# Group normalisation and a quantised 3x3 convolution: low parts by row pairs, and three steps on another engine

## The chip, the cores and the metric

The kernel runs on one core of one Trainium2 chip. The metric is the device time of one execution in microseconds (us). The engines are named as in the profile: PE (matmuls, with PEld for its weight loads), DVE (vector), ACT (scalar), POOL (GpSimd) and SP (which issues DMAs).

## What is computed

The input x has 160 images of 128 channels and 32x32 pixels; the weights U come in five sets (N = 5). Images go round the sets: image b*5 + n belongs to set n.

```python
beta, alpha = jnp.max(U), jnp.min(U)
s1 = (beta - alpha) / 3.0
v1 = s1 * floor(U / s1)
s2 = s1 / 5.0
v2 = s2 * floor((U - v1) / s2)
w = (v1 + v2).reshape(OUT_CH * N, IN_CH, 3, 3)
xb = _gn(x).reshape(B // N, N * C, H, W)      # 32 groups of 4 channels, each image for itself
act = conv(xb, w, stride 1, padding 1, feature_group_count=N)
out = x + act.reshape(x.shape)
```

## The kernel before, in words

Channels lie on the 128 partitions; an image is 1024 fp32 elements on each. The kernel goes through the images set by set, 32 images each. Four images make a chunk, loaded by one DMA of 2 MB from SP's queue (`load`, L304), 16 images ahead, and stored from ACT's queue after its fourth image (`residual`, L439).

The weights become small whole numbers m = 5*k1 + k2 in fp16, exact, with their scale kept for the end. `make_row` (L350) makes three of the nine taps of a set: 17 DVE operations on 384 elements (`quantise`, L93, and `floor_div`, L79; each yields after every operation, so that they can be dealt out), three transposes on PE (L364) and a copy by ACT (L366). Three such pieces make a set. For the first set they stand in the start; for each later one, from the 13th image of the set before on, four steps follow each image (`later`, L555 to L558), which takes 13 images.

An image passes through these steps:

- `measure` (L370): DVE's two `bn_stats` and one `bn_aggr` (L149, L150), 12 images ahead. Groups of 2, 2, 4, 4, 4 and then 8 images share what follows: `means` (L152, a matmul that averages the four channels of a group), `deviations` (L160, four small DVE operations), `variances` (L170, a matmul) and `scales` (L173: `ve` on DVE, a power and a product on POOL). Means and deviations fall to one image's turn, variances and scales to the next one's.
- `normalise` (L379): DVE makes z in fp32 (L384), ACT rounds it to fp16 (`hi`, L392).
- `remainder` (L395): DVE takes `lo` = z - `hi`, also fp16 (L398). `hi` + `lo` keep nearly all of z.
- `conv` (L400): for each tap, part (`hi`, `lo`) and half image (16 rows) one matmul of up to 512 columns, so 9 x 2 x 2 = 36, each with its own weight load, all into one pair of PSUM banks (`pc`, three pairs).
- `residual` (L424): DVE adds the scaled `pc` to x in place (L431).

The order of each engine's work is the order of the program text (`manual_schedule`). The loop of `run` (L519) puts for image i: means and variances, `normalise(i + 2)`, the 36 matmuls, `residual(i - 1)`, `remainder(i + 2)`, scales, deviations, one `measure`, four weight steps, a load. The start (L464 to L516) mixes the first set's weights with images 0 to 3 by hand; the first three images get their taps piece by piece as the weights come.

A general version for other weight ranges (`general_path`, L183) stands behind a test and doesn't run with these inputs.

## Time and profile before

| | |
|---|---|
| median of 3 runs | 1296.75 us (1295.84 to 1297.18) |
| profiled execution | 1296.91 us, span 1295.2 us |
| granted PE clock | 0.992 of full speed |
| busy: PE, DVE, ACT, POOL | 1238.0, 883.0, 174.6, 43.4 us |
| matmuls of the convolution (L416) | 5760 |
| DMA | 171.69 MB, mean 133 GB/s |

The span is the part of the time that the trace covers. A row of a group has the line, engine, operation, output and inputs, their shapes, the count, then busy us and mean ns of one, then the idle us just before them and who ended it. A matmul's duration covers its way through the array, in which the next one has begun; how fast they follow each other is read from their starts. In the timeline a row is a start, a length and what ran, like operations merged (x2); in the chain of waits a row is a stretch without a break.

### The profile page before, as it was taken

How to read it: one execution, taken by the hardware profiler on the slowest of the kernel's cores; microseconds unless marked ns; L12 is line 12 of the kernel's file. 1: busy time of each engine (PE TensorE's matmuls, PEld its weight loads, DVE VectorE, ACT ScalarE, POOL GpSimd, SP SyncE). 2: the span in 40 equal slices, each digit the busy share in tenths (PEclk: the TensorE clock that was granted, in tenths of full speed). 3: DMA queues.
4: the chain of work that ended last, by engine and by line, in shares of the span. 5: the costliest groups of instructions: out<-in, count | busy, mean ns of one | idle time of the engine just before them, and what ended most of it. 6: DMA issues, size and time to landing. Idle time of an engine off the chain costs nothing.

```text
span 1295.2 us, 13840 instructions
## 1 busy us (share of the span) xinstructions
PE 1238.0 (96%) x5901; PEld 580.1 (45%) x5901; DVE 883.0 (68%) x1367; ACT 174.6 (13%) x177; POOL 43.4 (3%) x57
## 2 busy tenths in 40 slices
PE   0589999999999999999999999999999999999997
PEld 0234444444444444444444444444444444444443
DVE  7886788855667887656688866657887566555441
ACT  0111111111111111111111111111111111111110
POOL 1000000000000000000000000000000000000000
PEclk9889999999999999999999999999999999999999
DMA  9403333333333333333333333433333333111122
GB/s 379 166 34 151 142 133 150 150 150 130 134 130 131 130 130 130 130 131 130 138 150 152 144 133 142 156 151 133 130 130 130 131 130 130 65 65 66 73 89 102
DMA packets 43270, 171.69 MB, mean 133 GB/s; under 512 B 1472, under 2 KB 1472, under 8 KB 43200
## 3 DMA queue, kind: packets, MB, share of 16 engines
q1 hardware_dynamic: 21600, 85.66, 17.8%
q10 hardware_dynamic: 21600, 85.07, 16.5%
q8 instruction: 48, 0.79, 0.2%
q14 instruction: 22, 0.18, 0.0%
HBM read 86.84 MB, written 83.89 MB: 132 GB/s over the span
## 4 chain that ended last, share of the span: by engine, by line
PE 94%; DVE 5%; DMA 0%; issue 0%; ACT 0%; DVEq 0%
PE pc L416 94%; DVE st L149 1%; DVE ext L323 0%; DVE ext L324 0%; DMA u<-in_L_conv_U_dram 0%; DVE tt L88 0%; DVE tt L89 0%; DVE tt L87 0%; DVE tt L90 0%; DVE k L91 0%; PE pg L156 0%; DVE z L384 0%; PE pg L171 0%; PE pt L364 0%; DVE lo L398 0%; DVE nn L85 0%
## 5 line engine op out<-in xcount | busy, mean ns | idle before, releaser
L416 PEld LDWEIGHTS <-wt 128*128 128x128 f16 x5760 | 565.4, 99 | 648.9 <-issue 7.5
L416 PE MATMUL pc<-hi,wt 128*128 128x496 f16 (+3 forms) x2880 | 850.3, 377 | 0.6 <-ACT wt L366 0.6
L416 PE MATMUL pc<-lo,wt 128*128 128x496 f16 (+3 forms) x2880 | 849.4, 376 | 0.0
L431 DVE SCALAR_TENSOR_TENSOR xt<-pc,s2z,xt 128x1024 f32<-128x1024 f32 (+1 forms) x161 | 205.5, 1277 | 370.4 <-PE pc L416 370.4
L392 ACT CAST hi<-z 128x1024 f16<-128x1024 f32 x160 | 167.2, 1045 | 984.0 <-DVE z L384 948.2
L149 DVE BATCH_NORM_STATS2 st<-xt 128x6 f32<-128x512 f32 x320 | 204.2, 680 | 0.0
L398 DVE TENSOR_TENSOR lo<-z,hi 128x1024 f16<-128x1024 f32 x160 | 194.5, 1216 | 4.0 <-ACT hi L392 4.0
L384 DVE TENSOR_SCALAR z<-xt,gm,rstd 128x1024 f32<-128x1024 f32 x160 | 125.2, 783 | 8.3 <-POOL rstd L180 8.2
L178 POOL TENSOR_TENSOR rstd<-ve,mhalf 128x8 f32<-128x8 f32 (+2 forms) x23 | 35.1, 1527 | 1163.0 <-DVE ve L176 1163.0
L150 DVE BATCH_NORM_AGGREGATE mv<-st 128x2 f32<-128x12 f32 x160 | 33.4, 209 | 5.5
L364 PE MATMUL pt<-ident,m 128*128 128x128 f16 x45 | 5.3, 231 | 19.2 <-DVE m L358 19.2
L366 ACT COPY wt<-pt 128x384 f16<-128x384 f16 x15 | 7.2, 478 | 102.1 <-DMA out_dram<-xt 59.4
L337 PE MATMUL rows<-ident,ext 128*1 128x128 f32 x2 | 0.6, 394 | 19.1 <-DVE ext L328 19.1
L90 DVE TENSOR_TENSOR tt<-tt,nn 128x384 f32<-128x384 f32 x30 | 16.5, 551 | 0.9
L91 DVE TENSOR_TENSOR k<-nn,tt 128x384 f32<-128x384 f32 x30 | 16.3, 544 | 0.7
L364 PEld LDWEIGHTS <-m 128*128 128x128 f16 x45 | 3.9, 106 | 22.2 <-DVE m L358 19.3
L156 PEld LDWEIGHTS pg<-mv,gavg 128*128 128x128 f32 x46 | 9.0, 202 | 8.6 <-DVE mv L150 5.0
L156 PE MATMUL pg<-mv,gavg 128*128 128x8 f32 (+2 forms) x46 | 7.1, 226 | 5.6 <-DVE mv L150 4.8
L171 PEld LDWEIGHTS pg<-dv,gavg 128*128 128x128 f32 x46 | 8.8, 202 | 7.6 <-DVE dv L168 5.2
L171 PE MATMUL pg<-dv,gavg 128*128 128x8 f32 (+2 forms) x46 | 7.3, 231 | 5.0 <-DVE dv L168 5.0
L86 DVE TENSOR_SCALAR nn<-nn 128x384 f32<-128x384 f32 x30 | 10.6, 352 | 0.8
L323 DVE TENSOR_REDUCE ext<-u 128x1 f32<-128x1152 f32 x5 | 6.7, 1344 | 5.1 <-DMA u<-in_L_conv_U_dram 5.1
(60 smaller groups left out, 130.1 us busy)
## 6 DMA issues: line engine op xcount, KB each, us to landing
xt<-in_x_dram SPq DMA_DIRECT2D x39, 2048.0 KB, 7.7
out_dram<-xt ACTq DMA_DIRECT2D x39, 2048.0 KB, 6.6
xt<-in_x_dram SPq DMA_DIRECT2D x4, 512.0 KB, 9.9
u<-in_L_conv_U_dram SPq DMA_DIRECT2D x3, 576.0 KB, 7.7
out_dram<-xt ACTq DMA_DIRECT2D x3, 512.0 KB, 2.6
u<-in_L_conv_U_dram ACTq DMA_DIRECT2D x2, 576.0 KB, 6.8
out_dram<-xt ACTq DMA_DIRECT2D x2, 256.0 KB, 2.9
```

The lines of the kernel that those rows point to most:

```text
L90: yield nc.vector.tensor_tensor(t, t, n, ALU.is_lt)
L91: yield nc.vector.tensor_sub(k, n, t)
L149: self.nc.vector.bn_stats(st[:, h, :], image[:, h * half : (h + 1) * half])
L150: self.nc.vector.bn_aggr(self.mv[:, j, :], st)
L156: self.nc.tensor.matmul(self.pg[:, 0, :], self.gavg, self.mv[:, :, 0], start=True, stop=True)
L171: self.nc.tensor.matmul(self.pg[:, 1, :], self.gavg, self.dv, start=True, stop=True)
L178: nc.gpsimd.tensor_tensor(self.rstd, ve, self.mhalf[:, : self.nb], ALU.pow)
L384: nc.vector.tensor_scalar(z, self.image(i), st.gm[:, j : j + 1], st.rstd[:, j : j + 1], ALU.subtract, ALU.mult,)
L392: nc.scalar.copy(hi.rearrange("p h w -> p (h w)"), z)
L398: self.nc.vector.tensor_sub(lo_flat, z, hi_flat)
L416: nc.tensor.matmul(pc[:, h, r0 - top : r1 - top, c0:c1], self.wts[n, tap // ROW][:, tap % ROW, :], self.pairs[i][part][:, r0 + dh : r1 + d ...
L431: self.nc.vector.scalar_tensor_tensor(xj[:, h], pc[:, h], self.steps.s2z, xj[:, h], ALU.mult, ALU.add)
```

## The change

From image 3 on, the low part is convolved two output rows at a time. With g0, g1, g2 the three taps of a column and x the low rows, the rows 2i and 2i+1 together need g0 on (x[2i-1] - x[2i+1]), -g2 on (x[2i] - x[2i+2]), and half the sum and half the difference of (g0+g1+g2) on (x[2i] + x[2i+1]) and (g0-g1+g2) on (x[2i+1] - x[2i]): four products for two rows, where the taps taken one by one need six. So DVE makes the row differences `d` and the sums and differences `st` (`combinations`), POOL the two weight combinations, ACT the negated g2. PE runs for an image six full-size matmuls on `st` into a bank pair `m` of its own, the 18 direct ones of the high part and twelve half-size ones on `d` (8 rows of 32) into `eo`. ACT brings `m` out as fp16 (`leave`), DVE makes its sum and difference by rows (`pq`, in `add_pairs`), and two matmuls with the scaled identity `up` add them to `eo`. Images 0 to 2 keep the direct form (`conv_direct`), image 2 in the bank pair `m`.

z is made on ACT from POOL's `shift` and `rstd`, three images ahead. Images with odd numbers get their sums and squares from two ACT operations (`image_sum`, `image_square`), with POOL operations between. Weights are made by columns of taps instead of rows. Output DMAs are issued by SP. The quantised weights of two sets are kept, not of five; x has six chunks, not seven. The test for the general version uses 40 in place of 128.

Statistics, pools and constants:

```diff
+    def image_sum(self, j, image, junk):
+        nc = self.nc
+        total = self.tile("total", [1])
+        nc.scalar.activation(junk, image, ACTF.Copy, accum_out=total)
+        minus = self.minus[j] = self.tile("minus", [1])
+        nc.gpsimd.tensor_scalar_mul(minus, total, -1.0 / image.shape[1])
+        nc.gpsimd.tensor_scalar_mul(self.mv[:, j, 0:1], total, 1.0 / image.shape[1])
...
+    def image_square(self, j, image, junk):
...
+        nc.scalar.activation(
+            junk, image, ACTF.Square, bias=self.minus[j], accum_out=squares
+        )
+        nc.gpsimd.tensor_scalar_mul(self.mv[:, j, 1:2], squares, 1.0 / image.shape[1])
...
+        self.shift = self.tile("shift", [self.nb])
+        nc.gpsimd.tensor_tensor(self.shift, self.gm, self.rstd, ALU.mult)
+        nc.gpsimd.tensor_scalar_mul(self.shift, self.shift, -1.0)
...
-    LEAD = 2
-    STAT_LEAD = 12
-    LOAD_LEAD = 16
...
+    STAT_LEAD = 13
+    LOAD_LEAD = 17
...
-        self.qpool = pool("quant", 2)
-        self.xpool = pool("x", 7)
...
+        self.qpool = pool("quant", 1)
+        self.wpool = pool("weights", 2)
+        self.xpool = pool("x", 6)
...
+        self.rows = pool("rows", 3)
+        self.evac = pool("evac", 2)
...
-        self.ps_conv = pool("ps_conv", 3, space=PSUM)
+        self.ps_eo = pool("ps_eo", 2, space=PSUM)
+        self.ps_m = pool("ps_m", 1, space=PSUM)
```

The parts of an image:

```diff
-        un = self.us[n][:, :, ROW * row : ROW * row + ROW]
...
+        un = self.us[n].rearrange("o i (r c) -> o i r c", c=ROW)[:, :, :, col]
...
+        wt = self.wpool.tile([P, 6, P], MM, tag=f"wt{col}", name=f"wt{n}_{col}")
+        nc.scalar.copy(wt[:, self.G, :], pt)
+        nc.scalar.mul(wt[:, self.MINUS_G2, :], pt[:, 2, :], -1.0)
+        outer = self.qpool.tile([P, P], MM, tag="outer", name=f"outer{n}_{col}")
+        nc.gpsimd.tensor_tensor(outer, wt[:, 0, :], wt[:, 2, :], ALU.add)
+        nc.gpsimd.tensor_tensor(wt[:, self.SUM, :], outer, wt[:, 1, :], ALU.add)
+        nc.gpsimd.tensor_tensor(wt[:, self.DIFF, :], outer, wt[:, 1, :], ALU.subtract)
+        self.wts[n, col] = wt
...
+        if i % 2 == 0:
+            st.image(j, image)
+            return
+        for s in stages:
+            junk = self.evac.tile([self.P, 1024], MM, tag="junk", name=f"junk{i}_{s}")
+            (st.image_sum, st.image_square)[s](j, image, junk)
...
-        nc.vector.tensor_scalar(
-            z, self.image(i), st.gm[:, j : j + 1], st.rstd[:, j : j + 1],
-            ALU.subtract, ALU.mult,
-        )
...
+        nc.scalar.activation(
+            z, self.image(i), ACTF.Identity,
+            bias=st.shift[:, j : j + 1], scale=st.rstd[:, j : j + 1],
+        )
+        self.z[i] = z
+    def high_part(self, i):
+        hi = self.parts.tile([self.P, self.H, self.W], MM, tag="hi", name=f"hi{i}")
+        self.nc.scalar.copy(hi.rearrange("p h w -> p (h w)"), self.z[i])
+        self.hi[i] = hi
...
+    def low_part(self, i):
+        lo = self.los[i % len(self.los)]
+        self.nc.vector.tensor_sub(
+            lo[:, 1 : self.H + 1, :].rearrange("p h w -> p (h w)"),
+            self.z.pop(i),
+            self.hi[i].rearrange("p h w -> p (h w)"),
+        )
+        return lo
...
+    def combinations(self, i):
...
+        d = self.rows.tile([P, H, W], MM, tag="d", name=f"d{i}")
+        st = self.rows.tile([P, 2, H // 2, W], MM, tag="st", name=f"st_{i}")
+        nc.vector.tensor_sub(d, lo[:, 0:H, :], lo[:, 2 : H + 2, :])
+        pairs = lo[:, 1 : H + 1, :].rearrange("p (i a) w -> p a i w", a=2)
+        nc.vector.tensor_add(st[:, 0], pairs[:, 0], pairs[:, 1])
+        nc.vector.tensor_sub(st[:, 1], pairs[:, 1], pairs[:, 0])
+        self.v[i] = (d, st)
...
+    def taps(self, i, part, col, target, last):
...
+        for k in (1, 0, 2):
+            for h in range(2):
+                h0 = h * (H // 2)
+                r0, r1 = max(h0, 1 - k), min(h0 + H // 2, H + 1 - k)
+                s0 = r0 + k - 1 + top
+                nc.tensor.matmul(
+                    target[:, h, r0 - h0 : r1 - h0, c0:c1],
+                    self.wts[n, col][:, k, :],
+                    tile[:, s0 : s0 + r1 - r0, c0 + dw : c1 + dw],
+                    start=(col == self.COLS[0] and k == 1 and top == 0),
+                    stop=(last and k == 2),
+                )
...
+    def conv_direct(self, i, col):
+        if i not in self.eo:
+            self.eo[i] = self.banks(*((self.ps_eo, "eo") if i < 2 else (self.ps_m, "m")), i)
+        self.taps(i, (self.hi[i], 0), col, self.eo[i], False)
+        lo = self.los[i % len(self.los)]
+        self.taps(i, (lo, 1), col, self.eo[i], col == self.COLS[-1])
...
+    def conv(self, i):
...
+        m = self.m[i] = self.banks(self.ps_m, "m", i)
+        for a, kind in enumerate((self.SUM, self.DIFF)):
+            for col in self.COLS:
+                product(
+                    m[:, a], kind, st[:, a], col, col == self.COLS[0], col == self.COLS[-1]
+                )
+        eo = self.eo[i] = self.banks(self.ps_eo, "eo", i)
+        for col in self.COLS:
+            self.taps(i, (self.hi[i], 0), col, eo, False)
+            for a, kind in enumerate((0, self.MINUS_G2)):
+                for h in range(2):
+                    rows = slice(h * 16 + a, h * 16 + 16, 2)
+                    to = eo[:, h].rearrange("p (i a) w -> p i a w", a=2)[:, :, a, :]
+                    product(to, kind, d[:, rows, :], col, False, False)
...
+    def leave(self, i):
+        m = self.evac.tile([self.P, 2, 512], MM, tag="mm", name=f"mm{i}")
+        self.nc.scalar.mul(m, self.m.pop(i).rearrange("p a i w -> p a (i w)"), DOWN)
+        self.m[i] = m
...
+    def add_pairs(self, i):
...
+        pq = self.evac.tile([self.P, 2, 512], MM, tag="pq", name=f"pq{i}")
+        rows = pq.rearrange("p h (i a w) -> p (h i) a w", a=2, w=self.W)
+        nc.vector.tensor_add(rows[:, :, 0], m[:, 0], m[:, 1])
+        nc.vector.tensor_sub(rows[:, :, 1], m[:, 0], m[:, 1])
+        for h in range(2):
+            to = self.eo[i][:, h].rearrange("p r w -> p (r w)")
+            nc.tensor.matmul(to, self.up, pq[:, h], start=False, stop=True)
...
+        xj = self.image(i)
+        self.nc.vector.scalar_tensor_tensor(
+            xj, eo.rearrange("p h r w -> p (h r w)"), self.steps.s2z, xj,
+            ALU.mult, ALU.add,
+        )
+        if i >= self.imgs - NB:
+            self.nc.sync.dma_start(self.ov[n, :, b, :], self.image(i))
+        elif i % NB == NB - 1:
+            self.nc.sync.dma_start(
```

The start:

```diff
+        self.measure(1)
         self.measure(0)
         next(over)
-        self.measure(1)
...
+        self.high_part(1)
+        self.measure(3)
+        take(column, 6)
+        self.low_part(0)
+        run(column)
+        self.low_part(1)
         self.measure(2)
-        self.measure(3)
...
+        self.conv_direct(0, 1)
+        self.conv_direct(1, 1)
         self.stats[1].means()
...
+        column = self.make_column(0, 0)
+        take(column, 2)
...
+        take(column, 4)
...
-        take(row, 4)
...
+        self.high_part(2)
+        self.normalise(3)
+        self.high_part(3)
+        take(column, 6)
+        self.low_part(2)
+        run(column)
+        self.conv_direct(2, 1)
...
+            self.conv_direct(i, 0)
+        column = self.make_column(0, 2)
         for i in range(4, 8):
             self.measure(i)
-        ready, measured, loaded, later = [self.stats[2]], 8, 3, None
-        middle = []
+        self.stats[2].means()
+        take(column, 6)
+        self.stats[2].deviations()
+        self.stats[2].variances()
+        take(column, 6)
+        self.stats[2].scales()
+        run(column)
+        ready, middle, measured, loaded, later = [], [], 8, 3, None
```

The loop (of which `measure`'s bookkeeping and the weight steps stay):

```diff
-            if self.FIRST + 1 <= i + self.LEAD < self.imgs:
-                self.normalise(i + self.LEAD)
             if i < self.FIRST:
-                self.conv(i, 2)
-            elif not final:
-                for r in range(len(self.ROWS)):
-                    self.conv(i, r)
+                self.conv_direct(i, 2)
             else:
...
-                for h in range(2):
-                    for r in range(len(self.ROWS)):
-                        self.conv(i, r, (h,))
-            if i > 0:
+                self.conv(i)
+            ahead = i + 10 if i < 8 else min(2 * i + 4, i + self.STAT_LEAD + 1)
+            to_measure = range(measured, min(self.imgs, ahead))
+            measured += len(to_measure)
+            if self.FIRST < i + 3 < self.imgs:
+                self.normalise(i + 3)
+            for k in to_measure:
+                if k % 2:
+                    self.measure(k, (0,))
+            if i >= self.FIRST:
+                self.leave(i)
+            if self.FIRST < i + 3 < self.imgs:
+                self.high_part(i + 3)
+            if self.FIRST <= i + 2 < self.imgs:
+                self.low_part(i + 2)
+                self.combinations(i + 2)
+            if i >= self.FIRST:
+                self.add_pairs(i)
+            if i < self.FIRST:
+                self.residual(i)
+            elif i > self.FIRST:
                 self.residual(i - 1)
...
-            if self.FIRST + 1 <= i + self.LEAD < self.imgs:
-                self.remainder(i + self.LEAD)
...
-            ahead = i + 9 if i < 8 else min(2 * i + 2, i + self.STAT_LEAD + 1)
-            while measured < min(self.imgs, ahead):
-                self.measure(measured)
-                k = self.group_of[measured]
-                measured += 1
-                if measured == self.groups[k].stop:
-                    ready.append(self.stats[k])
+            for k in to_measure:
+                self.measure(k, (1,))
+                group = self.group_of[k]
+                if k + 1 == self.groups[group].stop:
+                    ready.append(self.stats[group])
             if b == self.per_set * 3 // 8 and n + 1 < N_SETS:
-                later = (s for row in (1, 0, 2) for s in self.make_row(n + 1, row))
+                later = (s for col in self.COLS for s in self.make_column(n + 1, col))
             if later is not None:
                 take(later, 4)
                 if b == self.per_set - 1:
```

Two places in the order of DVE. The first is in the start, around the third piece of the first set's weights (names ending in `_2_` and a number: `tt`, `k`, `v`, `rest` are its steps, `m` its last). Before, the piece's last two steps, then the statistics of images 4 to 7 (`st`, `mv`), then the first of the deviations of their group (`gm`, which reads the result `pg` of the means matmul):

```order
L91 TENSOR_TENSOR k_0_2_392<-nn_2_389,tt_2_390 128x384
L358 SCALAR_TENSOR_TENSOR m_2_388<-k_0_2_391,k_0_2_392 128x384
L149 BN_STATS st_0_425<-xt_107 128x6 x2
L150 BN_AGGR mv_424<-st_0_425 128x2
L149 BN_STATS st_1_429<-xt_107 128x6 x2
L150 BN_AGGR mv_424<-st_1_429 128x2
L149 BN_STATS st_2_433<-xt_107 128x6 x2
L150 BN_AGGR mv_424<-st_2_433 128x2
L149 BN_STATS st_3_437<-xt_107 128x6 x2
L150 BN_AGGR mv_424<-st_3_437 128x2
L164 COPY gm_455<-pg_441 128x4
```

Now, from the sixth step of the piece on:

```order
L92 TENSOR_TENSOR tt_2_467<-tt_2_467,nn_2_466 128x384
L185 COPY gm_478<-pg_463 128x4
L187 TENSOR_TENSOR dv_480<-mv_434,gm_478 128x4
L188 TENSOR_TENSOR dv_480<-dv_480 128x4
L189 TENSOR_TENSOR dv_480<-dv_480,mv_434 128x4
L93 TENSOR_TENSOR k_0_2_468<-nn_2_466,tt_2_467 128x384
L104 TENSOR_SCALAR v_0_2_470<-k_0_2_468,s_189 128x384
L105 TENSOR_TENSOR rest_2_471<-u_101,v_0_2_470 128x384
```

The group's deviations have moved from behind the piece into its middle, and on PE the means matmul that they read now stands behind the 48 matmuls of images 0 to 2 (before: also behind the piece's transposes).

The second place is in the loop, during image 88, where the third piece of the weights of the set from image 96 on ends. Before, one image's turn (`z`, residual, `lo`, statistics, weight steps):

```order
L384 TENSOR_SCALAR z_5116<-xt_4322,gm_4924,rstd_4999 128x1024
L431 SCALAR_TENSOR_TENSOR xt_4127<-pc_5069,s2z,xt_4127 128x1024
L398 TENSOR_TENSOR lo_5119<-z_5116,hi_5118 128x1024
L149 BN_STATS st_4_5161<-xt_5010 128x6 x2
L150 BN_AGGR mv_4930<-st_4_5161 128x2
L90 TENSOR_TENSOR tt_2_4945<-tt_2_4945,nn_2_4944 128x384
L91 TENSOR_TENSOR k_3_2_4947<-nn_2_4944,tt_2_4945 128x384
L358 SCALAR_TENSOR_TENSOR m_2_4943<-k_3_2_4946,k_3_2_4947 128x384
```

Now:

```order
L444 TENSOR_TENSOR lo_138<-z_6540,hi_6544 128x1024
L458 TENSOR_TENSOR d_6617<-lo_138 128x1024
L460 TENSOR_TENSOR st_6618<-lo_138 128x512
L461 TENSOR_TENSOR st_6618<-lo_138 128x512
L540 TENSOR_TENSOR pq_6622<-mm_6612 128x16x32
L541 TENSOR_TENSOR pq_6622<-mm_6612 128x16x32
L551 SCALAR_TENSOR_TENSOR xt_5231<-eo_6509,s2z,xt_5231 128x1024
L92 TENSOR_TENSOR tt_2_6359<-tt_2_6359,nn_2_6358 128x384
L93 TENSOR_TENSOR k_3_2_6361<-nn_2_6358,tt_2_6359 128x384
L392 SCALAR_TENSOR_TENSOR m_2_6357<-k_3_2_6360,k_3_2_6361 128x384
```

z is gone, and `d`, two `st` and two `pq` stand ahead of the residual and of the piece's last steps; an even image's turn has no statistics on DVE. On PE the piece's transposes stand behind the image's two `up` matmuls, in both versions at the end of the same image.

129 lines of the change are left out of this document (50 added, 79 removed).

## The prediction

> **What bounds the kernel now.** I read the page first: how busy each engine is, then the chain that ended last.
>
> ```profile
> PE 1238.0 (96%) x5901; PEld 580.1 (45%) x5901; DVE 883.0 (68%) x1367; ACT 174.6 (13%) x177; POOL 43.4 (3%) x57
> ...
> PE 94%; DVE 5%; DMA 0%; issue 0%; ACT 0%; DVEq 0%
> ```
>
> A busy PE need not be a PE at its limit, so the chain, in order of time, is the better witness. This piece is seven images without a break:
>
> ```profile
> 345.84 53.36 PE pc L416 x252
> ```
>
> 53.36 / 7 = 7.62 us per image of 36 matmuls, with nothing between them. The groups say who waits for whom:
>
> ```profile
> L431 DVE SCALAR_TENSOR_TENSOR xt<-pc,s2z,xt 128x1024 f32<-128x1024 f32 (+1 forms) x161 | 205.5, 1277 | 370.4 <-PE pc L416 370.4
> L392 ACT CAST hi<-z 128x1024 f16<-128x1024 f32 x160 | 167.2, 1045 | 984.0 <-DVE z L384 948.2
> L149 DVE BATCH_NORM_STATS2 st<-xt 128x6 f32<-128x512 f32 x320 | 204.2, 680 | 0.0
> L398 DVE TENSOR_TENSOR lo<-z,hi 128x1024 f16<-128x1024 f32 x160 | 194.5, 1216 | 4.0 <-ACT hi L392 4.0
> L384 DVE TENSOR_SCALAR z<-xt,gm,rstd 128x1024 f32<-128x1024 f32 x160 | 125.2, 783 | 8.3 <-POOL rstd L180 8.2
> L90 DVE TENSOR_TENSOR tt<-tt,nn 128x384 f32<-128x384 f32 x30 | 16.5, 551 | 0.9
> L86 DVE TENSOR_SCALAR nn<-nn 128x384 f32<-128x384 f32 x30 | 10.6, 352 | 0.8
> L366 ACT COPY wt<-pt 128x384 f16<-128x384 f16 x15 | 7.2, 478 | 102.1 <-DMA out_dram<-xt 59.4
> ```
>
> DVE waits 370 us for PE and PE waits for DVE only at the start: PE is the bound, DVE has a third of the span free, ACT most of it.
>
> **The change: products.** What one matmul takes is read from the starts in the timeline of PE (full-size ones, then three transposes of 128 columns with a weight load each, and what follows them):
>
> ```profile
> 1005.42 0.59 PE L416 MATMUL pc<-hi,wt 128*128 128x512 f16 x2
> 1005.85 0.59 PE L416 MATMUL pc<-lo,wt 128*128 128x512 f16 x2
> 1006.28 0.59 PE L416 MATMUL pc<-hi,wt 128*128 128x496 f16 x2
> ...
> 1008.01 0.58 PE L416 MATMUL pc<-hi,wt 128*128 128x480 f16 x2
> ```
>
> ```profile
> 990.01 0.33 PE L364 MATMUL pt<-ident,m 128*128 128x128 f16 x3
> 990.18 0.59 PE L416 MATMUL pc<-hi,wt 128*128 128x512 f16 x2
> ```
>
> 512 columns: 0.43 / 2 = 0.215 us. Eight of 16 rows of 31: (1008.01 - 1006.28) / 8 = 0.216, so a short row costs as much as a full one. 128 columns: 0.17 / 3 = 0.057. No row has 256 columns; it lies between 0.057 and 0.215, and I take the line through both, 0.057 + 128/384 x 0.158 = 0.110. An image from the fourth on then has 18 high-part matmuls of the old mix (7.62 / 36 = 0.212 each: 3.81), six sums and two `up` of full size (8 x 0.216 = 1.73) and twelve half-size ones (1.32): 6.86 us, 0.763 less. For 157 images: **-119.8 us**.
>
> **The change: DVE's load.** From one start to the next in its timeline:
>
> ```profile
> 999.20 1.21 DVE L398 TENSOR_TENSOR lo<-z,hi 128x1024 f16<-128x1024 f32 x1
> 1000.34 1.28 DVE L149 BATCH_NORM_STATS2 st<-xt 128x6 f32<-128x512 f32 x2
> 1001.65 0.21 DVE L150 BATCH_NORM_AGGREGATE mv<-st 128x2 f32<-128x12 f32 x1
> 1001.77 0.76 DVE L384 TENSOR_SCALAR z<-xt,gm,rstd 128x1024 f32<-128x1024 f32 x1
> ...
> 1005.62 1.28 DVE L431 SCALAR_TENSOR_TENSOR xt<-pc,s2z,xt 128x1024 f32<-128x1024 f32 x1 [3.09 <-PE pc L416]
> 1006.82 1.22 DVE L398 TENSOR_TENSOR lo<-z,hi 128x1024 f16<-128x1024 f32 x1
> ```
>
> `lo` takes 1.14, the statistics of an image 1.43, the residual 1.20; an operation hides 0.08 of its duration under the next. Gone are the normalisation and every second image's statistics. New are five all-16-bit tensor-tensor operations: `d` of 1024 elements, two sums and two `pq` of 512. No row shows one. The upper end is the rows of the same kind: L398 and L90 give (1216 - 551) / 640 = 1.04 ns an element and 152 ns fixed, so 1.216 and four of 0.684, or 3.55 us with 0.08 off each. The lower end is the row that shows DVE doing better than that: L384 against L86 gives (783 - 352) / 640 = 0.673 ns an element, with 8 bytes moved for each; the new ones move 6, so 0.505 and the fixed 152: 0.669 and four of 0.411, or 1.91 us. I take the lower: in bytes, which the new operations halve, L384 is the nearer row. With 0.12 for `d`, which must wait for `lo`, DVE has 1.14 + 1.20 + 0.72 + 0.12 + 1.91 = 5.09 us per image, and 6.73 at the upper end: both under 6.86. So PE stays the bound on most images either way.
>
> The Trainium skill (VectorE: DVE Perf Modes, "The perf-mode tier table") says that a tensor-tensor operation on 16-bit SBUF data runs two elements a cycle (1224 ns for 2048), and only fp32 one. By it 1024 cost about 0.69 us (an estimate from that page), and the sum below would be the same within 2 us; by the same-kind rows it would be 79 to 103 us higher (rival 1). No row here shows a 16-bit case.
>
> **The change: images with quantisation.** For 13 images of each of four sets, DVE also does four quantising steps:
>
> ```profile
> 963.65 0.57 DVE L87 SCALAR_TENSOR_TENSOR tt<-nn,s1hi,u 128x384 f32<-128x384 f32 x1
> ...
> 966.04 0.81 DVE L384 TENSOR_SCALAR z<-xt,gm,rstd 128x1024 f32<-128x1024 f32 x1
> ...
> 971.13 0.50 DVE L91 TENSOR_TENSOR k<-nn,tt 128x384 f32<-128x384 f32 x1
> ...
> 973.05 0.81 DVE L384 TENSOR_SCALAR z<-xt,gm,rstd 128x1024 f32<-128x1024 f32 x1
> ```
>
> Four take 2.39 or 1.92, 2.15 on average: 7.24 us per image, over PE's 6.86. Two images (one with statistics) need 14.5 against 13.7: DVE falls 0.8 behind per pair, and 1.1 on the first. After twelve images that is 1.1 + 5 x 0.83 = 5.3. PE meets it where a column ends: its transposes stand behind the image's last `up` and wait for DVE's `m`. Without lag `m` comes 6.1 into the image (sums 1.3, drain 0.17, `leave` 1.05, `pq` 0.7, residual 1.2, up to three steps 1.6), PE is there at 6.86: a cushion of 0.75. So about 4.5 per set, **+18 us** in four; at the upper end, with 8.88 us per image, 12 x 2.02 - 0.75 = 23.5 per set, 94. Before, these transposes waited twice in all, both times in the start:
>
> ```profile
> PE pt L364 <- DVE m L358: 19.2, 2, 9.9
> ```
>
> **The change: the start.**
>
> ```profile
> 45.56 0.16 DVE L164 COPY gm<-pg 128x2 f32<-128x2 f32 x1 [2.98 <-PE pg L156]
> ...
> 56.01 0.56 DVE L358 SCALAR_TENSOR_TENSOR m<-k,k 128x384 f16<-128x384 f32 x1
> ...
> 67.14 0.56 DVE L358 SCALAR_TENSOR_TENSOR m<-k,k 128x384 f16<-128x384 f32 x1
> ...
> 68.25 0.33 PE L364 MATMUL pt<-ident,m 128*128 128x128 f16 x3
> ...
> 73.37 0.59 PE L156 MATMUL pg<-mv,gavg 128*128 128x4 f32 x2 [4.79 <-DVE mv L150]
> ```
>
> ```profile
> 74.00 0.16 DVE L164 COPY gm<-pg 128x4 f32<-128x4 f32 x1 [0.68 <-PE pg L156]
> ...
> 74.67 1.28 DVE L149 BATCH_NORM_STATS2 st<-xt 128x6 f32<-128x512 f32 x2
> ...
> 80.18 0.15 DVE L176 TENSOR_SCALAR ve<-pg 128x4 f32<-128x4 f32 x1
> ```
>
> ```profile
> 73.96 4.98 PE pc L416 x12
> 79.16 13.04 PE pc L416 x60
> ```
>
> Up to the second column's `m` (56.6) I expect the same within 1 us: three normalisations and a statistic leave DVE, waits for the high parts through POOL and ACT come in. Then the group-2 means matmul stands on PE behind 48 matmuls that end at about 68.2, and DVE's copy `gm` now stands in the middle of the third column, six steps in. DVE waits there (as at 45.56, 2.98), with 11 steps (2.15 / 4 = 0.54 each, 5.9), the deviations (74.67 - 74.00 = 0.67) and `ve` (0.15) behind it: `m` ends at 75.1 in place of 67.7, transposes and weight copy (L366, 0.48) 1.0, first matmul 76.1 against 73.96. Twelve matmuls take 4.98 there (half speed after the wait), so image 0 ends at 81.3. Then DVE runs residual, statistics, low part with combinations (2.55), residual, statistics, 2.55, residual = 11.6 us (1.20 + 1.43 + 2.55 + 1.20 + 1.43 + 2.55 + 1.20) before image 3 may begin, because image 2 sits in the one `m` bank pair: 92.9. Before it began at 79.16 + 24 x 0.212 = 84.2. **+8.7**; PE has then idled 6 us, and 4.98 in place of 2.54 for the next dozen shows what that costs: **+2**.
>
> **At nothing.** ACT: four or five passes of about 1.05 (L392) are 4.2 us, a quarter more if the accumulating ones cost more, under 6.86; exposed, each 0.1 us per image would be 16 us. `leave` stands behind a normalisation that waits for POOL's scales once in eight images; 3 us lie between `pq` and `up`. Output DMAs move from ACT's queue to SP's, ahead of loads:
>
> ```profile
> xt<-in_x_dram SPq DMA_DIRECT2D x39, 2048.0 KB, 7.7
> ```
>
> A load held up by one image (6.9) and 7.7 to land is still inside the three images, 20.6 us, to its first reader.
>
> **Sum.** The profiled execution took 1296.91 with a span of 1295.2 and stands 0.16 from the median of the runs, so nothing is corrected: 1296.9 - 119.8 + 18 + 10.7 = **1206 us**.
>
> **Rivals.** (1) *Sixteen-bit operations at one element a cycle.* For it: the rows of the same kind, L398 and L90. Against: L384. Quantisation 94 in place of 18, start +3: 1285; waits of 4 us and more then fall at every column's end, and at 2 us for the slow clock behind each of twelve, 1309. Near 1297, no change or slower. (2) *Half-size products at full price*, on the slower side: if the weight load of each isn't hidden or alternate PSUM rows cost, twelve of them at 0.215 add 157 x 12 x 0.105 = 198, less the 18 that DVE then has time for: 1386. It decides from 0.110 + 90.9 / 1884 = 0.158 us each. Against it: transposes at 0.057 with a load each. The Trainium skill (TensorE: Matmul & The Clock Gate, "LDWEIGHTS") puts a load of 128 columns at about 107 ns, which, if it ran bare, would be this rival; the transposes show that it does not. (3) *The scalar chain*: `leave` comes late on every image by some 0.3 us beyond its cushion: +47, 1253. (4) *The start and the lag cost nothing*: 1177.
>
> **Chances.** Forecast 0.77 (its own range 1185 to 1225, the upper part for the price of L384's row uncut, 0.78 and 0.44: +10), rival 4 0.05, rival 3 0.05, rival 1 0.08, rival 2 0.05. The range that leaves out two in ten goes from 1182 to 1245, taking in half-size products up to 0.13. A measurement of this kernel can tell about 0.2%, 2.6 us, from no change. Faster by more: forecast, 3 and 4, and some of rival 1: 0.90. Slower: rival 2 and half of rival 1: 0.08. Within: 0.02.
>
> **What would show it.** Right: images 6.86 us apart where no quantising runs; the half-size group 0.11 apart; the five new DVE groups near 0.67 and 0.41; PE idle before L398's transposes at the second and third column's end of a set; image 3 starting near 93; ACT under 75% busy. Wrong: `d` at 1.2 (rival 1), images at 8 us with DVE waiting for PE (rival 2), `up` waiting for `pq` on plain images (rival 3).

## The result, and the profile after

| | before | after |
|---|---|---|
| median | 1296.32 us (1295.84 to 1297.18, 4 runs) | 1238.57 us (1235.40 to 1238.82, 4 runs) |
| ratio, 95% interval | | 0.9548 (0.9532 to 0.9565) |
| profiled execution, span | 1296.91, 1295.2 us | 1238.82, 1237.1 us |

The change is faster by 57.8 us, not by the 91 that were forecast: 1206 was said, 1238.6 came, inside the range. The page of after, busy time and the chain that ended last:

```profile
PE 1134.9 (92%) x6215; PEld 612.2 (49%) x6215; DVE 979.9 (79%) x1751; ACT 678.1 (55%) x829; POOL 234.7 (19%) x392
...
PE 62%; DVE 31%; POOL 3%; issue 2%; ACT 1%; DMA 0%; DVEq 0%; POOLq 0%
```

Before, the chain was PE for 94% and DVE for 5. Now DVE holds 31% of it, although it is busy in only 79% of the span and PE in 92: there must be stretches in which the two wait for each other. Busy time by stretch shows where. The columns are the stretch, its length, and the busy time (and instructions) of PE, PEld, DVE, ACT and POOL; then the granted PE clock, the DMA share and GB/s. The first stretch is images 33 to 40, where nothing is quantised. Quantising begins with image 44 (the thirteenth of its set) and ends in image 56; the second stretch is images 48 to 57, from the first column's end to the image behind the third:

```profile
319.47:374.56 55.09, 55.09 (x309) 30.23 (x308) 41.58 (x74) 33.45 (x40) 11.46 (x16) 1.00 0.41 153
422.80:503.88 81.08, 72.56 (x395) 38.29 (x393) 75.68 (x135) 43.67 (x56) 16.12 (x28) 0.98 0.40 147
```

Eight plain images take 55.09 us, 6.89 each, and PE is never idle. The ten of the second stretch take 81.08, 8.11 each; PE is busy for 72.56 of them and DVE for 75.68, so both stand idle: 8.5 and 5.4 us. From the starts of each image's first product, the distances in that stretch, in us (plain: 6.85, or 6.99 with a statistics matmul):

| image | 48 | 49 | 50 | 51 | 52 | 53 | 54 | 55 | 56 | 57 |
|---|---|---|---|---|---|---|---|---|---|---|
| after | 9.11 | 6.85 | 7.12 | 8.04 | 9.36 | 6.85 | 7.94 | 6.85 | 10.45 | 8.49 |

The long ones are 48, 52 and 56, where a column of weights ends, the image behind the third end (57), and 51 and 54. The waits view names the pairs (us in total, times, longest):

```profile
PE pt L398 <- DVE m L392: 48.9, 15, 11.4
...
PE eo L544 <- DVE pq L541: 7.6, 14, 0.9
```

```profile
DVE pq L540 <- ACT mm L531: 139.4, 103, 4.9
...
ACT z L431 <- POOL shift L205: 99.9, 22, 15.4
```

PE waits for the column at all 15 ends; 3 of them lie in the start, 12 in the loop, where before there was not one.

How an image with a column's end comes to take ten microseconds is seen in the timeline of all engines, image 56. Columns: start, duration, engine and line, operation; in brackets the idle time before it and who ended it:

```profile
494.54 0.56 DVE L392 SCALAR_TENSOR_TENSOR m<-k,k 128x384 f16<-128x384 f32 x1
...
495.16 0.44 PE L398 MATMUL pt<-ident,m 128*128 128x128 f16 x3 [2.26 <-DVE m L392]
...
495.39 2.77 PE L505 MATMUL m<-st,wt 128*128 128x512 f16 x6
495.64 0.48 ACT L400 COPY wt<-pt 128x384 f16<-128x384 f16 x1 [6.10 <-PE pt L398]
...
496.18 1.24 ACT L431 ACTIVATE z<-xt,shift,rstd 128x1024 f32<-128x1024 f32 x1
...
496.34 0.90 DVE L458 TENSOR_TENSOR d<-lo 128x1024 f16<-128x1024 f16 x1
496.77 0.75 POOL L404 TENSOR_TENSOR wt<-outer,wt 128x128 f16<-128x128 f16 x1
...
498.20 1.02 ACT L531 ACTIVATE mm<-m 128x1024 f16<-128x1024 f32 x1 [0.78 <-PE m L505]
...
499.25 0.42 DVE L540 TENSOR_TENSOR pq<-mm 128x512 f16<-128x512 f16 x1 [0.88 <-ACT mm L531]
```

Four queues, each in order. PE's transposes wait for DVE's `m`. ACT's weight copy waits for the transposes, and behind it in ACT's queue stand the normalisation and `leave`. PE's sums of the next image stand behind the transposes; `leave` needs them; and DVE, 0.9 us ahead of `leave`, stands idle for it at `pq`. What DVE is late by, PE loses; and what DVE stands, it is later by at the next end. The clock has a part in this one: from 495.16 to 498.20 it is granted at 0.52, the six sums take 2.77 us in place of 1.46, and ACT itself stands 0.78 for them before `leave`. Behind the ends in images 48 and 52, at full clock, DVE doesn't stand behind the weight copy.

The longer stands of DVE come from POOL's scales. At the end of image 52, POOL's power starts at 462.08, the shift ends at 466.22, `z` starts at 466.26, `leave`, behind it, at 467.40, and `pq` at 468.44, after DVE has stood 1.98 us. The same happens in image 45:

```profile
406.43 0.43 DVE L540 TENSOR_TENSOR pq<-mm 128x512 f16<-128x512 f16 x1 [1.65 <-ACT mm L531]
...
468.44 0.42 DVE L540 TENSOR_TENSOR pq<-mm 128x512 f16<-128x512 f16 x1 [1.98 <-ACT mm L531]
```

With the 0.88 at 499.25, DVE stands 4.5 us for `leave` in images 45 to 57.

### The profile page after: what moved, and what is told of

It is laid out like the page before. It is cut to its first block, busy times and chain, and to the rows that moved or that the text cites. A ratio compares the mean times of both kernels' runs of the same rounds, so it can differ in the third digit from the quotient of the medians.

```text
span 1237.1 us, 16052 instructions
## 1 busy us (share of the span) xinstructions
PE 1134.9 (92%) x6215; PEld 612.2 (49%) x6215; DVE 979.9 (79%) x1751; ACT 678.1 (55%) x829; POOL 234.7 (19%) x392
## 4 chain that ended last, share of the span: by engine, by line
PE 62%; DVE 31%; POOL 3%; issue 2%; ACT 1%; DMA 0%; DVEq 0%; POOLq 0%
PE eo L478 34%; PE m L505 12%; PE eo L505 11%; DVE xt L551 5%; DVE lo L444 4%; PE eo L544 4%; DVE st L152 3%; DVE d L458 2%; DVE pq L541 1%; POOL rstd L199 1%; DVE tt L91 1%; DVE pq L540 1%; DVE tt L92 1%; DVE st L460 1%; DVE tt L89 1%
## 5 line engine op out<-in xcount | busy, mean ns | idle before, releaser
L478 PE MATMUL eo<-hi,wt 128*128 128x512 f16 (+1 forms) x2862 | 690.9, 378 | 1.1 <-ACT wt L400 1.1
L531 ACT ACTIVATE mm<-m 128x1024 f16<-128x1024 f32 x157 | 160.3, 1021 | 353.3 <-PE m L505 353.1
L505 PE MATMUL eo<-d,wt 128*128 128x256 f16 (+1 forms) x1884 | 283.3, 273 | 0.0
L431 ACT ACTIVATE z<-xt,shift,rstd 128x1024 f32<-128x1024 f32 x160 | 198.1, 1238 | 99.9 <-POOL shift L205 99.9
L505 PE MATMUL m<-st,wt 128*128 128x512 f16 x942 | 235.2, 387 | 3.2 <-DVE xt L551 3.2
L551 DVE SCALAR_TENSOR_TENSOR xt<-eo,s2z,xt 128x1024 f32<-128x1024 f32 x159 | 202.9, 1276 | 8.4 <-PE eo L478 5.9
L444 DVE TENSOR_TENSOR lo<-z,hi 128x1024 f16<-128x1024 f32 x160 | 193.2, 1207 | 3.8 <-ACT hi L439 3.8
L540 DVE TENSOR_TENSOR pq<-mm 128x512 f16<-128x512 f16 x157 | 66.3, 422 | 144.3 <-ACT mm L531 139.4
L458 DVE TENSOR_TENSOR d<-lo 128x1024 f16<-128x1024 f16 x157 | 109.5, 697 | 58.8 <-PE eo L505 48.2
L152 DVE BATCH_NORM_STATS2 st<-xt 128x6 f32<-128x512 f32 x160 | 102.0, 679 | 0.0
L199 POOL TENSOR_TENSOR rstd<-ve,mhalf 128x8 f32<-128x8 f32 (+2 forms) x23 | 47.2, 2052 | 167.3 <-DVE ve L197 167.3
L460 DVE TENSOR_TENSOR st<-lo 128x512 f16<-128x512 f16 x157 | 67.5, 430 | 0.0
L461 DVE TENSOR_TENSOR st<-lo 128x512 f16<-128x512 f16 x157 | 66.5, 423 | 0.0
L541 DVE TENSOR_TENSOR pq<-mm 128x512 f16<-128x512 f16 x157 | 65.5, 417 | 0.0
```

The source lines that it names most:

```text
L152: self.nc.vector.bn_stats(st[:, h, :], image[:, h * half : (h + 1) * half])
L431: nc.scalar.activation(z, self.image(i), ACTF.Identity, bias=st.shift[:, j : j + 1], scale=st.rstd[:, j : j + 1],)
L444: self.nc.vector.tensor_sub(lo[:, 1 : self.H + 1, :].rearrange("p h w -> p (h w)"), self.z.pop(i), self.hi[i].rearrange("p h w -> p (h w)"),)
L458: nc.vector.tensor_sub(d, lo[:, 0:H, :], lo[:, 2 : H + 2, :])
L478: nc.tensor.matmul(target[:, h, r0 - h0 : r1 - h0, c0:c1], self.wts[n, col][:, k, :], tile[:, s0 : s0 + r1 - r0, c0 + dw : c1 + dw], start ...
L505: nc.tensor.matmul(target[:, :, c0:c1], self.wts[n, col][:, kind, :], source[:, :, c0 + dw : c1 + dw], start=start, stop=stop,)
```

## Experiments

**Theory**, once the two traces were compared: the step on quantising images failed. They cost not 4.5 but 12 us a set, because the lag is not carried along and paid once: in-order queues at the column ends (A) and `leave` behind the normalisation and POOL's scales (C) make PE and DVE wait by turns. **Rival** (B, load): DVE has simply more work than PE in these images, and PE would wait for it in one place or another, however it is ordered. A second rival: something else that falls on the same images.

All kernels below are the changed one with the edit shown. The changed kernel and e1 to e6 have the same start, and yet image 3 begins anywhere from 95.8 to 98.6 us in their profiled executions; so what a set loses is read from the image distances, beside the time.

| run | median, us | range | ratio to before, 95% interval |
|---|---|---|---|
| e1, no quantising in the loop | 1189.75 | 1188.39 to 1190.37 | 0.918 (0.9164 to 0.9195) |
| e2, column ends one image later | 1220.89 | 1219.59 to 1221.77 | 0.9419 (0.9403 to 0.9434) |
| e3, leave first | 1220.06 | 1220.03 to 1221.11 | 0.9418 (0.9402 to 0.9434) |
| e4, statistics 14 ahead | 1227.31 | 1226.72 to 1232.32 | 0.947 (0.9454 to 0.9486) |
| e5, these three edits together | 1210.04 | 1209.30 to 1210.69 | 0.9335 (0.9319 to 0.935) |
| e6, two steps per image | 1197.29 | 1196.59 to 1198.70 | 0.9238 (0.9223 to 0.9254) |
| e7, group 2 behind the start | 1231.87 | 1228.87 to 1232.41 | 0.9496 (0.948 to 0.9511) |
| e8, six products | 1305.08 | 1304.02 to 1305.96 | 1.007 (1.0053 to 1.0087) |
| e9, products alone | 1315.26 | 1314.56 to 1315.53 | 1.0145 (1.0129 to 1.016) |
| e10, all that helped | 1182.61 | 1180.67 to 1182.89 | 0.9119 (0.9107 to 0.9132) |

### e1: what the quantising costs in all

```diff
-                later = (s for col in self.COLS for s in self.make_column(n + 1, col))
+                self.wts.update({(n + 1, col): self.wts[0, col] for col in self.COLS})
```

> This kernel leaves out the quantisation of sets 1 to 4 (their images are convolved with the weights of set 0); the start and everything else stays. In the changed kernel the four quantising stretches cost 12 to 13 us each over the distance of plain images (6.85 and 6.99 us). If they are the whole excess over plain images, this gives 1238.6 - 4 x 12.3 = about 1190 us (1185 to 1196). If the excess belongs to something else that happens at the same images (loads, statistics, the group scales from POOL), the time stays over 1205.

1189.75. The same ten images, in the stretch view of e1:

```profile
409.63:478.43 68.80, 68.80 (x386) 37.67 (x384) 51.86 (x91) 41.82 (x50) 13.89 (x20) 1.00 0.45 166
```

68.80 in place of 81.08: 12.3 in this set. By the image distances the four sets lose 12.3, 12.3, 12.0 and 10.6, or 47 in all. The time fell by 48.8, because image 3 also begins 0.8 sooner and what follows the last image's start is 1.0 shorter. The loads, statistics and group scales are still there, so the second rival is out. (12 x 0.17 = 2 of the 47 are the transposes' own time on PE.)

### e2: the column ends one image later

```diff
+        def finish():
...
+            self.wts[n, col] = wt
+
+        self.ends.append(finish)
+        if not late:
+            self.ends.pop()()
...
-                later = (s for col in self.COLS for s in self.make_column(n + 1, col))
+                later = (s for col in self.COLS for s in self.make_column(n + 1, col, True))
...
+            if self.ends:
+                self.ends.pop(0)()
             if later is not None:
                 take(later, 4)
```

`finish` holds the transposes, the weight copies and POOL's sums of a column; it runs in the turn after the column's last step.

> The end of each column inside the loop (three transposes, two weight copies, three POOL sums) is issued one image later, so that on PE the transposes find the quantised column ready; the number of steps per image and their place on DVE stay. Theory A (waits on PE's in-order queue at the column ends): the three waits of 2.3, 2.5 and 3.6 us in each set go and only part comes back as waits for pq: 4 x -6 = about -24, 1214 us (1205 to 1224). Theory B (DVE has simply too much work in these 13 images; PE waits for it in one place or another): no change within 5 us, the waits of PE for the column turn into waits for pq or for the bank.

1220.89, 17.7 less: theory A's side, in the upper part of its range. The waits of PE in e2, and the ten images:

```profile
PE pt L399 <- DVE m L392: 28.6, 3, 11.4
PE eo L549 <- DVE pq L546: 20.8, 24, 1.5
```

```profile
417.54:494.02 76.48, 70.52 (x394) 38.05 (x393) 72.11 (x131) 40.69 (x51) 11.05 (x23) 1.00 0.37 136
```

The 20.3 us of waits at the 12 ends in the loop are gone whole (48.9 to 28.6, the three of the start). 13.2 came back as waits for `pq` (7.6 to 20.8). PE's busy time in the ten images fell too, from 72.56 to 70.52, with the granted clock at 1.00 in place of 0.98. So B is wrong as it was put, "no change", but its mechanism holds for a part.

### e3: leave ahead of the normalisation

```diff
+            if i >= self.FIRST:
+                self.leave(i)
             if self.FIRST < i + 3 < self.imgs:
                 self.normalise(i + 3)
...
-            if i >= self.FIRST:
-                self.leave(i)
```

> On the scalar engine the copy of the sums out of PSUM (leave) is issued ahead of the next normalisation in every image, in place of behind it and behind every second image's sum. Theory C (DVE stands idle for leave, up to 2 us at the twelfth and twentieth image of a set where the normalisation waits for POOL, and about 1 us behind each column end, and that idle time is what it lacks): 4 x -4 = -16, 1222 us. Theories A and B: within 5 us of 1238.6, since DVE's idle time there only mirrors what PE has waited for.

1220.06, 18.5 less, as theory C had it. In e3 the ten images take 7.5 over e1's in place of 12.3:

```profile
416.61:492.92 76.31, 72.06 (x394) 38.25 (x393) 73.59 (x130) 44.35 (x56) 15.03 (x28) 0.98 0.40 147
```

```profile
PE eo L544 <- DVE pq L541: 1.1, 4, 0.3
```

No column end was moved, yet the four sets lose 4.6, 4.8, 5.0 and 2.0 us less by the distances, and in the second set DVE stands 0.33 us for `leave` in images 45 to 57 where it stood 4.5: its idle time for `leave` did not merely mirror PE's. (Single images go both ways: the one behind the third end fell from 8.49 to 6.85 in the second set and rose from 6.85 to 8.29 in the fourth.)

### e4: statistics one image further ahead

```diff
-    STAT_LEAD = 13
+    STAT_LEAD = 14
```

> Statistics run one image further ahead (14 in place of 13), so that POOL's scales (power, factor, two shift operations, about 4.2 us) have a whole image before the first normalisation that reads them; nothing else changes. If the late scales are part of the excess (twice in each quantising stretch, about 1 us each): 4 x -2 = -8, about 1231 us. If they only take up time that PE or DVE wait for anyway: within 3 us of 1238.6.

1227.31, 11.3 less, a little more than expected. In the waits view of e4 ACT stands for POOL 5 times in place of 22:

```profile
ACT z L431 <- POOL shift L205: 40.2, 5, 15.4
```

Images 51 and 54 went from 8.04 and 7.94 to 6.85, while image 52 went from 9.36 to 10.38: what is saved in one place is partly paid at the next column's end. (The profiled execution of e4 took 1232.32, the longest of its four, and its distances show 6.6 of the 11.3; from 461.9 to 468.8, around the end of image 52, its clock is granted at 0.51, and image 53 went from 6.85 to 9.67.)

### e5: do they add up?

The three edits together.

> The three edits together: column ends one image later, leave ahead of the normalisation, statistics 14 ahead; still four quantising steps per image in the same 13 images. Alone they took 17.7, 18.5 and 11.3 us off the changed kernel. If each removes waits of its own, they add up to -47.5: about 1191 us, and the excess of the quantising stretches is gone. If they take away the same idle time, because DVE's load in these images (14.8 us per pair against PE's 13.85) stays over PE's and only the cushion is larger: 6.2 us of lag per set less 3 of cushion remain, about 1202 us, hardly under the best two of them.

1210.04: neither. They do not add up (28.5 in place of 47.5), and 20.3 us stay over e1, more than the 12 that the load was priced at. The ten images, and the first and the last of nine low parts in the timeline of DVE in e5:

```profile
413.60:487.56 73.96, 70.53 (x396) 38.20 (x395) 71.56 (x129) 43.66 (x54) 13.64 (x26) 1.00 0.40 144
```

```profile
408.80 1.22 DVE L449 TENSOR_TENSOR lo<-z,hi 128x1024 f16<-128x1024 f32 x1
...
469.16 1.22 DVE L449 TENSOR_TENSOR lo<-z,hi 128x1024 f16<-128x1024 f32 x1
```

Between them DVE stands for nothing: eight images in 60.36 us, 7.55 each, against 6.89 of PE. This is the load alone. 13 x (7.55 - 6.89) = 8.6 per set are to be caught up, and 73.96 - 68.80 = 5.2 were lost: a cushion of 3.4, about the 3 us between `pq` and `up`. The load was forecast at 7.24. Of the 0.31 more, four steps take 2.24 on average in place of 2.15 (the ones that read the weights column by column are dearer), the deviations of a group (0.9 once in eight images, 0.11) had been left out, and the rest lies in `lo`, `d`, `st` and `pq` and their gaps.

### e6: less load, same order

```diff
-            if b == self.per_set * 3 // 8 and n + 1 < N_SETS:
+            if b == self.per_set // 8 and n + 1 < N_SETS:
...
-                take(later, 4)
+                take(later, 2)
```

> Two quantising steps per image from the fifth image of a set on, in place of four from the thirteenth; everything else as in the changed kernel (the column ends in place, leave behind the normalisation). DVE then has 6.3 us per image, half a microsecond under PE. Theory load (DVE over PE's pace in these images is what lets the waits form): the excess of 49 us goes nearly whole, about 1193 us (1190 to 1198). Theory order (the column end and leave cost by where they stand, whatever the load): at least the three column ends of a set keep 1 to 2 us each, 1205 to 1214.

1197.29: 41 of the 48.8 are gone, near what the load theory said, and of the 12 column ends in the loop only four still wait, the third of each set. The timeline of e6 at image 29, a third column's end:

```profile
280.54 1.24 ACT L431 ACTIVATE z<-xt,shift,rstd 128x1024 f32<-128x1024 f32 x1 [4.33 <-POOL shift L205]
...
282.73 0.42 DVE L540 TENSOR_TENSOR pq<-mm 128x512 f16<-128x512 f16 x1 [1.98 <-ACT mm L531]
...
286.60 0.35 PE L398 MATMUL pt<-ident,m 128*128 128x128 f16 x3 [1.11 <-DVE m L392]
```

There the late scales and the column's end fall into one image. DVE is under its load, and still ACT waits for POOL, DVE for ACT and PE for DVE; that image takes 8.31 in place of 6.85. So order costs something without the load, but without the load it can be caught up within an image.

### e7: the start

```diff
-        self.stats[2].means()
-        take(column, 6)
-        self.stats[2].deviations()
-        self.stats[2].variances()
-        take(column, 6)
-        self.stats[2].scales()
         run(column)
-        ready, middle, measured, loaded, later = [], [], 8, 3, None
+        self.stats[2].means()
+        self.stats[2].deviations()
+        ready, middle, measured, loaded, later = [], [self.stats[2]], 8, 3, None
```

> The means and deviations of the third group of images stand behind the third column of the start, as they did before the change, and its variances and scales in the first turn of the loop; nothing else changes. In the changed kernel DVE stands 6.8 us in the middle of that column, because the means stand on PE behind 48 matmuls. If that wait is the cost of the start: third column ready at 72.9 in place of 80.5, image 3 at about 90 in place of 97.9, time about 1231 us. If PE's slow clock or the three residuals and low parts behind it set the start anyway: within 3 us of 1238.6.

1231.87, 6.7 less. The chain in order of time (start, duration, what), first of after, then of e7:

```profile
60.81 4.77 PE m L478 x12
...
81.57 4.74 PE eo L478 x12
86.34 1.28 DVE xt L551
...
97.90 2.72 PE m L505 x6
```

```profile
60.40 4.54 PE m L478 x12
...
74.99 2.58 PE eo L478 x12
77.59 1.28 DVE xt L551
...
89.22 2.72 PE m L505 x6
```

The matmuls of the third column begin 6.6 us sooner and run at full pace (2.58 for twelve in place of 4.74), image 3 begins 8.7 sooner. Of this, 0.5 is lost again in image 3 itself and 1.7 in the last two quantising stretches. The wait in mid-column is the cost that it was said to be.

### e8 and e9: each half of the change alone

e8 keeps the normalisation and half of the statistics on ACT and takes the old six products:

```diff
-            self.eo[i] = self.banks(*((self.ps_eo, "eo") if i < 2 else (self.ps_m, "m")), i)
+            self.eo[i] = self.banks(*((self.ps_eo, "eo") if i != 2 else (self.ps_m, "m")), i)
...
-            if i < self.FIRST:
-                self.conv_direct(i, 2)
-            else:
-                self.conv(i)
+            for col in (2,) if i < self.FIRST else self.COLS:
+                self.conv_direct(i, col)
...
-                self.leave(i)
...
-                self.combinations(i + 2)
...
-                self.add_pairs(i)
```

> One half of the change alone: normalisation and every second image's statistics on the scalar engine as in the changed kernel, but all images with six products for the low part as before (no combinations, no leave, no up). PE has the matmuls of the kernel before, 7.62 us per image, and DVE much less work. By the step 'start' it should cost what the start costs and no more: third column 7.6 us later than before (81.6 against 74.0), about 1304 us, a little slower than before (1299 to 1308). If the normalisation on the scalar engine hinders more than that (late scales, z and hi in a row), over 1310.

1305.08, as the start alone had it. In the loop PE doesn't stand; ten images:

```profile
422.80:503.00 80.20, 80.20 (x388) 37.61 (x387) 55.20 (x84) 31.60 (x42) 10.73 (x25) 1.00 0.30 113
```

e9 takes the new products and puts normalisation and all statistics back on DVE:

```diff
-        self.shift = self.tile("shift", [self.nb])
-        nc.gpsimd.tensor_tensor(self.shift, self.gm, self.rstd, ALU.mult)
-        nc.gpsimd.tensor_scalar_mul(self.shift, self.shift, -1.0)
...
-        if i % 2 == 0:
+        if 0 in stages:
             st.image(j, image)
-            return
+        return
...
-        nc.scalar.activation(
-            z, self.image(i), ACTF.Identity,
-            bias=st.shift[:, j : j + 1], scale=st.rstd[:, j : j + 1],
+        nc.vector.tensor_scalar(
+            z, self.image(i), st.gm[:, j : j + 1], st.rstd[:, j : j + 1],
+            ALU.subtract, ALU.mult,
         )
...
-            for k in to_measure:
-                if k % 2:
-                    self.measure(k, (0,))
...
-                self.measure(k, (1,))
+                self.measure(k)
```

> The other half of the change alone: four products with their combinations, leave and up as in the changed kernel, but normalisation and all statistics on DVE as before. DVE per plain image: lo 1.14, residual 1.20, statistics 1.43, normalisation 0.69, five new operations 1.95, d's wait 0.12: 6.53 us, still under PE's 6.85, so plain images stay 6.85 us apart. In the quantising images 2.4 more: about 8.9 us, 2.0 over PE in 13 images, less 3 of cushion: 23 per set, 92 over the kernel without quantisation (1189.75): about 1280 us (1270 to 1300). If the scalar engine's share of the change was not needed for that gain (waits only, as with the edits above), it stays at 1240 or below.

1315.26, slower than before and 15 over the top of the expectation. Plain images are 6.85 us apart, as expected. Its ten images:

```profile
453.16:546.85 93.69, 77.49 (x394) 39.61 (x393) 90.78 (x160) 22.10 (x26) 9.56 (x11) 0.91 0.36 135
```

DVE is busy in 97% of the stretch, the load theory's picture; 24.9 over e1 here and 3.0 in images 46 and 47, 28 per set in place of 23, with the granted clock at 0.91. The start costs 8 more (image 3 at 105.3 against 97.1 in e1) and images 10 and 11 another 6. 4 x 28 + 8 + 6 = 126 over e1, and 125.5 were measured. So the halves alone are 0.7% and 1.5% slower than before, and together they are 4.5% faster.

### e10: all that helped

e2 to e4, e6 and e7 together, and the first three residuals ahead of the low part of the image two further on:

```diff
+            if i < self.FIRST:
+                self.residual(i)
             if self.FIRST <= i + 2 < self.imgs:
                 self.low_part(i + 2)
                 self.combinations(i + 2)
             if i >= self.FIRST:
                 self.add_pairs(i)
-            if i < self.FIRST:
-                self.residual(i)
-            elif i > self.FIRST:
+            if i > self.FIRST:
                 self.residual(i - 1)
```

> All that helped, together: two quantising steps per image from the fifth on, column ends one image later, leave ahead of the normalisation, statistics 14 ahead, the third group's means behind the third column of the start, and the first three residuals ahead of the low part of the image two further on, so that image 2's bank comes free sooner. If the excess of the quantising stretches is load and order and nothing else, the kernel without quantisation (1189.75) less 6.7 (start) less 2.5 (one low part with combinations out of the way of image 3): about 1181 us (1178 to 1187). If the edits share what they save, as three of them did, about 1190 us.

1182.61, 56 us under the change as made (0.9119 of before against 0.9548). PE waits for a column twice, both times in the start:

```profile
PE pt L399 <- DVE m L392: 22.8, 2, 11.4
```

Behind image 3, which takes 9.67, no image takes over 7.02, a plain one with its three transposes (6.85 + 0.17). Image 3 begins at 87.4, and 1189.75 less (97.1 - 87.4) plus 12 x 0.17 is 1182.1: the excess is gone.

## Why the prediction was right and where it was wrong

**Products: right.** Image distances on plain images are 6.85 (6.86 said). Two rows of the timeline of PE in after show the half-size product:

```profile
434.48 0.60 PE L505 MATMUL eo<-d,wt 128*128 128x256 f16 x4
434.92 1.43 PE L478 MATMUL eo<-hi,wt 128*128 128x496 f16 x6
```

Four start within 0.44 us, 0.110 each, as taken from the line through the two known sizes. Rival 2 falls with it.

**DVE's price: right.** The groups of after, mean ns behind the busy time:

```profile
L458 DVE TENSOR_TENSOR d<-lo 128x1024 f16<-128x1024 f16 x157 | 109.5, 697 | 58.8 <-PE eo L505 48.2
...
L460 DVE TENSOR_TENSOR st<-lo 128x512 f16<-128x512 f16 x157 | 67.5, 430 | 0.0
...
L540 DVE TENSOR_TENSOR pq<-mm 128x512 f16<-128x512 f16 x157 | 66.3, 422 | 144.3 <-ACT mm L531 139.4
```

0.697 and 0.42 to 0.43 against 0.669 and 0.411: the size was 4% short at most, rival 1 is out. The reason given for the size is not shown, and that it came so near is in part luck: by bytes `lo` (4 and 2 read, 2 written) would go at the 0.673 ns an element of L384, which also moves 8, and it takes 1207 ns for 1024. The Trainium skill (VectorE: DVE Perf Modes, "The perf-mode tier table") gave, as an estimate, about 0.69 for 1024 elements by its two elements a cycle; the trace agrees.

**Quantising images: the step that failed.** It said 18 us; the distances put it at 47, or 45 without the transposes' own 2. (By its own rows the 18 should be 16: 14.48 less 13.72 is 0.76 a pair, not 0.83, and the parts of the 6.1 add up to 6.0.) The statement "PE meets it where a column ends ... about 4.5 per set" took the lag for a debt that DVE's work alone makes and that is paid once, at the last end, against a cushion of 0.75. Two things in it were off:

1. The load. An image takes DVE 7.55 us (e5), not 7.24, so the lag per set is 8.6 and not 5.3.
2. `leave` behind a normalisation that waits for POOL was put "at nothing", because it happens once in eight images and 3 us lie between `pq` and `up`. The cushion is there, but in the quantising images the lag had already used it up, and every stand of DVE is added to the lag. Over the same thirteen images (45 to 57 and their like) DVE stands 4.1, 4.5, 4.5 and 3.6 us for `leave` in the four sets, each time 3.6 of it behind POOL's shift. The rest, 2.2 us in all, stands behind three of the twelve column ends.

An estimate for the second set from these traces, with the prediction's cushion: 8.6 - 0.75 + 4.5 = 12.35, and 12.3 were measured. For e3, with 0.33 of standing, it gives 8.2 (7.5 measured); for e4, with 2.6, 10.4 (10.5); for e2, with the 3.4 of cushion that e5 shows and 3.6 of standing, 8.8 (7.7). So ending a column later pays by a larger cushion, and `leave` first and earlier statistics pay by less standing; the estimate is good to about 1 us a set. With both gone 20 us remain (e5), near the 18 said, but by another route: a larger lag against a larger cushion. Of the 28.5 that e5 saves, 27 lie in the four sets and 1.7 in the start.

PE's clock has a share that wasn't tried by itself. In the loop of the changed kernel it is granted at half five times, for 3.4 us each, each time about a column's end; at half pace that is 1.7 us of work each, 8.5 in all at most. In the loops of e2, e5 and e6 this doesn't happen.

**Start: the mechanism right, the size short.** 10.7 was said. Image 3 begins at 97.90 in place of 84.4 and takes 9.37 in place of 6.85: 16.0. The step "up to the second column's `m` the same within 1 us" is the one that failed: `m` ended at 60.25 against 56.57. The chain of after, then that of before, shows why:

```profile
51.15 1.05 POOL rstd L199
...
53.71 1.25 ACT z L431
54.98 1.05 ACT hi L439
56.06 1.23 DVE lo L444
```

```profile
53.13 1.13 DVE lo L398
```

Image 2's low part, with the column's last steps behind it, waits for POOL's scales and shift, `z` and `hi` in a row: 2.9 us later. The 48 matmuls behind that column, and the means behind them, moved with it; they end at 73.2, 5.0 later than said, because the first twelve also take 4.77 us where twelve at full pace take 2.54. The step behind it held: from the end of image 0's matmuls to image 3, 11.6 us were said, and 97.90 - 86.34 is 11.56; e7 shows the mid-column wait by itself.

The sum by the measured sizes, for the profiled executions: 1296.9 before, -120.9 for the products (157 x 0.77), +16.0 for the start, +45 for the quantising and +1.7 behind the last image's start, which the prediction didn't have, is 1238.7; 1238.8 were measured.

**Rival 3** named the engine rightly (`leave` late) and the images wrongly: on plain images `up` doesn't wait. **At nothing** was right for ACT's load (55% busy) and SP's queue: no wait for a load appears on the chain of the loop.

## What to carry to other kernels

When an engine goes from a third idle to nearly full in some stretch (here DVE, 75.7 of 81.1 us), the work that is dealt out beside the main stream must be spread anew: here four steps per image had room before and none after, and two per image over twice as many images gave back 41 us without another edit. The lag between two in-order engines is not only the late one's excess of work. Follow what stands ahead of its inputs on every other queue: each stand of the late engine is added to its lag, and the other engine pays for it at the next place where they meet. Issuing the consumer one turn later makes the cushion larger, and issuing the shared step first takes the stand away. And price a shared helper (here POOL's scales) against the cushion in the worst stretch, not in the average one.

## What the runs showed of the hardware that was not expected

DVE and POOL take longer side by side. In the rows of image 56 above, `d` took 0.90 us while POOL made its weight sums (0.697 on average), and POOL's sum 0.75, where the same sum took 0.43 beside a waiting DVE (at 467.00, in image 53). POOL's one-element products average 678 and 660 ns, its power 2052 against 1527 before; whether a busy DVE is the cause there wasn't tried. The Trainium skill (SBUF — State Buffer, "SBUF: two separate sides") says that the two engines take one port pair by an exclusive lock when DVE has two SBUF inputs; the durations are in keeping with it, and no run here shows the lock itself.

The clock fell after one pair of short stops and not after another. The timeline of PE in after, at the ends of images 48 and 56:

```profile
430.06 0.59 PE L544 MATMUL eo<-pq,up 128*128 128x512 f16 x2 [0.68 <-DVE pq L541]
431.73 0.35 PE L398 MATMUL pt<-ident,m 128*128 128x128 f16 x3 [1.07 <-DVE m L392]
431.91 1.46 PE L505 MATMUL m<-st,wt 128*128 128x512 f16 x6
...
492.31 0.59 PE L544 MATMUL eo<-pq,up 128*128 128x512 f16 x2 [0.79 <-DVE pq L541]
```

After 0.68 and 1.07 us of standing the next six products take 1.46 us; after 0.79 and 2.26, at image 56, they take 2.77, half pace. In the stretch view of after, the third number from the end is the granted clock:

```profile
495.16:498.20 3.04, 3.04 (x10) 1.29 (x11) 2.94 (x4) 1.79 (x4) 1.75 (x3) 0.52 1.02 399
431.91:433.37 1.46, 1.46 (x10) 0.69 (x8) 1.39 (x4) 1.26 (x3) 0.69 (x1) 1.00 0.86 331
```

In after, each accumulating pass of ACT brings a read of the accumulator of 0.19 us with it, and the normalisation with two per-channel operands takes 1238 ns where the cast of the same size takes 1037. Both were inside the allowance for ACT.
